# The head of a GRU kernel: the order of its first loads and products

## The chip, the cores and the metric

The kernel runs on one core of one Trainium2 chip. The metric is device time in microseconds (us) from the start to the end of one launch; the smaller the better. A profile of one execution is at hand beside the times.

## The reference

A recurrent network (a GRU cell) runs over 256 time steps for a batch of 16 sequences of width 512; its states then go through an expert layer with a router, and the result is added to the input. Cut to what matters here:

```python
def cell(h, x):                       # 256 times, one after the other
    gi = x @ W_ih + b_ih              # known for all steps ahead of time
    gh = h @ W_hh + b_hh              # needs the state of the step before
    i_r, i_z, i_n = jnp.split(gi, 3, axis=-1)
    h_r, h_z, h_n = jnp.split(gh, 3, axis=-1)
    r = jax.nn.sigmoid(i_r + h_r)
    z = jax.nn.sigmoid(i_z + h_z)
    n = jnp.tanh(i_n + r * h_n)
    return (1.0 - z) * n + z * h
# h starts as cond (16 x 512); W_ih and W_hh are 512 x 1536, x is 16 x 256 x 512
# then: logits = hs @ router_w + router_b; softmax over 16 experts; each expert
# takes its 256 best tokens; y adds weight * (token @ expert_w + expert_b)
# result: x + y
```

All tensors are float32.

## The kernel before

**Stages.** The kernel has three: a head that loads the weights and works out the first input products, a loop of 256 recurrence steps, and an end that picks the tokens of each expert and writes the result. The change touches the head alone.

**Layout.** The time steps are cut into 32 groups of 8 (TG = 8, NG = 32); group g of x lies in `xs[:, g]`, 128 rows (16 sequences by 8 steps) of 512 values. W_ih lies in `wih`, four blocks k = 0 to 3 of 128 rows of 1536 values (0.79 MB each, one contiguous row of 6 KB for each partition); W_hh lies in `whh`, loaded by gate (r, z and n are gates 0, 1 and 2; 1 MB each, in pieces of 2 KB). `b_raw` and `b_n` hold the bias vectors, `c0` the first state. Parts of `xs` that are not yet needed serve as room for other things: the bias vectors, the masks' numbers, and sums made from W_ih.

**What the head does on TensorE (PE).** `begin_sums` (L93) multiplies zeros to open six PSUM banks, and two more such products (`keep_clock`, 512 columns each) follow. `spread_x(0)` transposes group 0 (four products with `ident`, L732), and VectorE (DVE) copies the result to `xT[0]` in four parts (L735). Two more `keep_clock` products follow. Then come the input products (L618) of W_ih's blocks k = 0 to 3, for four pairs of time steps each; behind block 1 the transposes of `c0` (L748); behind block 2 the bias products (`biases`, L492: 16 products of one or two rows of ones with the bias vectors, which spread the biases over the partitions) and the transposes of group 1 (L732). After block 3 come the products of two more pairs of steps, one more `keep_clock` product, and the first recurrence products of the loop (L705).

**What the head does on the other engines.** DVE makes the masks (`make_masks`, from numbers that GpSimd (POOL) writes), the copies of x, sums and differences of W_ih's blocks (`mixes`, L645, 1.75 us each at full size), the copy of the biases (L756, L757), and adds the biases to the products (`x_done`, L629). ScalarE (ACT) is used in the head for DMA issues and, at its end, for four small copies.

**Queues.** Three engines issue DMAs: ACT and SP (SyncE) through hardware queues, POOL through a software queue; in the profile they are q10, q1 and q0. ACT issues group 0 of x, blocks 0 and 1 of W_ih, gate 0 of W_hh and three quarters of gate 1. SP issues blocks 2 and 3, group 1 of x, gate 2, the last quarter of gate 1, and group 2 of x in 8 pieces (`load_xa`). POOL issues `cond` and three bias vectors. A one-element POOL write into block 2 (L457) makes SP wait until POOL has come that far.

**What sets the order.** The blocks under `manual_schedule` keep the order in which the code is written, for the engines named there, so each engine runs its instructions in the order of the text and waits by semaphores. A DMA whose issue follows eight or more others also waits for the landing of an earlier one, since eight semaphores go round for the hardware queues.

Of the kernel before, what the change touches and what calls it, by code (L numbers as in the profile page):

```python
# [11 lines left out]
I32 = mybir.dt.int32  # L12
AF = mybir.ActivationFunctionType
ALU = mybir.AluOpType
# [3 lines left out]
def kernel(  # L18
# [15 lines left out]
    nc = tc.nc  # L34
    B, T, D = x.shape
    E = router_w.shape[1]
    P = 128
    QD = 32
    KC = D // P
    TG = P // B  # L40
# [5 lines left out]
    xs = const.tile([P, NG, D], F32, name="xs")  # L46
# [4 lines left out]
    wih = const.tile([P, KC, 3, D], F32, name="wih")  # L51
# [6 lines left out]
    GH = P // E  # L58
# [7 lines left out]
    ones_b = const.tile([P, B], F32, name="ones_b")  # L66
    zero = xs[:, NG - 1, D - P // 2 :].bitcast(BF16)
    nc.gpsimd.memset(zero, 0.0)
    make_identity(nc, ident)

    def make_masks():

        nc.gpsimd.memset(ones_b, 1.0)
        shift = GH.bit_length() - 1
        at = xs[:, 10, 0:3].bitcast(I32)
        nc.gpsimd.iota(at[:, 0:1], pattern=[[0, 1]], base=0, channel_multiplier=1)
        nc.vector.tensor_single_scalar(at[:, 1:2], at[:, 0:1], shift, ALU.logical_shift_right)
        nc.vector.tensor_single_scalar(at[:, 2:3], at[:, 0:1], GH - 1, ALU.bitwise_and)
        at_f = xs[:, 11, 0:3]
        nc.vector.tensor_copy(at_f, at)  # L80
        to_i = xs[:, 11, P : 3 * P].bitcast(I32).rearrange("p (o e h) -> p o e h", o=2, h=GH)
        nc.gpsimd.iota(to_i[:, 0, :, :], pattern=[[1, E], [0, GH]], base=0, channel_multiplier=0)
        nc.gpsimd.iota(to_i[:, 1, :, :], pattern=[[0, E], [1, GH]], base=0, channel_multiplier=0)
        to = xs[:, 10, P : 3 * P].rearrange("p (o n) -> p o n", o=2)
        nc.vector.tensor_copy(to, to_i.rearrange("p o e h -> p o (e h)"))
        nc.vector.tensor_scalar(same_f, to[:, 0, :], at_f[:, 1:2], None, ALU.is_equal)
        nc.vector.tensor_copy(same_h, same_f)
        nc.vector.tensor_scalar(row_of, to[:, 1, 0:GH], at_f[:, 2:3], None, ALU.is_equal)
# [273 lines left out]
    with (  # L362
# [12 lines left out]
        whh = wts.tile([P, KC, 3, D], F32, name="whh")  # L375
        bias = wts.tile([P, 4, P], F32, name="bias")
# [4 lines left out]
        C2 = 3 * P // 2  # L381
        spare = xs[:, RING:, :].rearrange("p g d -> p (g d)")[:, AHEAD * 3 * P : AHEAD * 3 * P + C2]
# [9 lines left out]
        c0 = xs[0:B, 7, :]  # L392
# [18 lines left out]
        def load_xa(g, xa, j, qs):  # L411

            for o in range(2):
                q = QD * j + B * o
                qs[o].dma_start(
                    out=xa[q : q + B],
                    in_=x[:, g * TG + o : (g + 1) * TG : 2, j * P : (j + 1) * P],
                )
# [7 lines left out]
        def new_xa():  # L426
            return xap.tile([P, TG // 2, P], F32, name="xa")
# [12 lines left out]
        with tc.manual_schedule(engines={ET.SP, ET.Activation, ET.Pool}):  # L440
            def load_gate(gate, queue, ks=slice(0, KC)):
                queue.dma_start(
                    out=whh[:, ks, gate, :],
                    in_=w_hh[:, gate * D : (gate + 1) * D].rearrange("(c p) n -> p c n", c=KC)[:, ks, :],
                )

            def load_k(k, queue):
                queue.dma_start(
                    out=wih[:, k].rearrange("p g d -> p (g d)"),
                    in_=w_ih.rearrange("(p c) n -> p c n", c=KC)[:, k, :],  # L450
                )

            nc.scalar.dma_start(out=xs[:, 0, :], in_=x[:, 0:TG, :])
            load_k(0, nc.scalar)
            load_k(1, nc.scalar)
            nc.gpsimd.dma_start(out=c0, in_=cond)
            nc.gpsimd.memset(wih[0:1, 2, 0, 0:1], 0.0)  # L457
            load_k(2, nc.sync)
            load_k(3, nc.sync)
            nc.sync.dma_start(out=xs[:, 1, :], in_=x[:, TG : 2 * TG, :])  # L460
            load_gate(0, nc.scalar)
            load_gate(2, nc.sync)
            load_gate(1, nc.scalar, slice(0, KC - 1))
            load_gate(1, nc.sync, slice(KC - 1, KC))
            xa_next = new_xa()
            for c in range(KC):
                load_xa(2, xa_next, c, (nc.sync, nc.sync))
            nc.scalar.activation(dummy, ones[0:1, 0:1], AF.Sigmoid)
            for dst, src in (
                (b_raw[0:1], b_ih.rearrange("(o g d) -> o g d", o=1, d=D)),  # L470
                (b_raw[1:2], b_hh.rearrange("(o g d) -> o g d", o=1, d=D)),
                (b_n, b_hh[2 * D :].rearrange("(o d) -> o d", o=1)),
            ):
                nc.gpsimd.dma_start(out=dst, in_=src)

        def load_expert(part, s):

# [11 lines left out]
        def biases(bank):  # L489
            for i, rows in enumerate((b_raw[:, 0, :], b_raw[:, 1, :], b_raw[0:1, 2, :], b_n)):  # L490
                for j in range(KC):
                    nc.tensor.matmul(  # L492
                        bank[quadrant(j), P * i : P * (i + 1)],
                        ones[0 : rows.shape[0]],
                        columns(rows, j),
                        start=False,
                        stop=True,
                        tile_position=(0, QD * j),
                        skip_group_check=True,
                    )  # L500
# [216 lines left out]
        def keep_clock(n, banks=idles):  # L717

            for i in range(n):
                begin_sums(banks[i % len(banks)])  # L720

        with tc.manual_schedule(engines={ET.PE, ET.Activation, ET.DVE, ET.Pool}):
            make_masks()
            for bank in banks:
                begin_sums(bank)
            keep_clock(2)
            held = (r_bank, n_bank, z_bank, x_bank0, x_bank1, idles[1])

            def spread_x(g, bank):
                xT[g] = xtp.tile([P, TG // 2, P], F32, name="xt")  # L730
                for c in range(KC):
                    nc.tensor.transpose(bank[:, P * c : P * (c + 1)], xs[:, g, c::KC], ident)  # L732
                for q in range(TG // 2):
                    to = xT[g][:, q, :].rearrange("p (c o b) -> p c o b", c=KC, b=B)
                    nc.vector.tensor_copy(  # L735
                        to, bank.rearrange("p (c b t) -> p c t b", c=KC, t=TG)[:, :, 2 * q : 2 * q + 2, :]
                    )

            spread_x(0, idles[0])
            keep_clock(2, (idles[1],))  # L740
            for k in range(KC):
                for p in range(KC):
                    for gates in (slice(0, 1), slice(1, 3)) if p == k == 0 else (slice(0, 3),):
                        x_part(p, k, held[p], gates, start=False)
                if k == 1:
                    mixes(0)
                    for c in range(KC):
                        nc.tensor.transpose(  # L748
                            idles[0][:, B * c : B * (c + 1)], c0[:, P * c : P * (c + 1)], ident[0:B, 0:B]
                        )  # L750
                    nc.vector.tensor_copy(
                        hs[:, :, 0, :], idles[0][:, 0 : KC * B].rearrange("p (k b) -> p k b", b=B)
                    )
                elif k == 2:
                    biases(l_bank)
                    nc.vector.tensor_copy(bias, l_bank.rearrange("p (g d) -> p g d", d=P))  # L756
                    nc.vector.tensor_tensor(spare, bias_f[:, C2 : 2 * C2], bias_f[:, 0:C2], ALU.subtract)  # L757
                    spread_x(1, idles[0])
                    x_sums(1)
                elif k == 3:  # L760
                    mixes(1)
            for p in range(KC):
                x_done(p, held[p])
                if p == 0:
                    preset_first(0)
                elif p == 2:
                    preset_rest(0)
            for p in (KC, KC + 1):
                for k in range(KC):
                    for gates in (slice(0, 1), slice(1, 3)):  # L770
                        x_part(p, k, held[p], gates, start=False)
                if p == KC:
                    mixes(3)
                x_done(p, held[p])
                if p == KC:
                    nc.scalar.copy(a_sum, bias_f[:, 0:C2])
            keep_clock(HEAD_FILL, (idles[0],))

        first, second = range(KC // 2), range(KC // 2, KC)

        with tc.manual_schedule(engines={ET.PE, ET.Activation, ET.DVE, ET.Pool, ET.SP}):
# [6 lines left out]
            for s in range(T):  # L788
# [25 lines left out]
                n = 0  # L814
# [451 lines left out]
```

## Time and profile before

| | us |
|---|---|
| median of 3 runs (lowest, highest) | 1114.81 (1114.41, 1114.88) |
| the profiled execution: time, and span of its instructions | 1114.45, 1112.6 |
| PE busy | 1101.7 (99%) |
| PE's recurrence products, L705 | 722.1 |
| DVE busy | 802.0 (72%) |
| ACT busy | 579.0 (52%) |
| POOL busy | 30.0 (3%) |
| start of the loop (first L705) in the span | 25.79 |

The span goes from the first to the last instruction that the profile shows. PE is busy nearly throughout; the granted TensorE clock is 0.998 of full speed over the span. In the first fortieth of the span the DMA engines are busy 7 tenths and move 258 GB/s, in the second 63 GB/s: the head is the stage that loads. Line numbers (L618) are those of the kernel before; where the changed kernel is meant, the text says so.

### The profile page before, as it was taken

The page shows a single profiled execution, that of the slowest core. Times are in us where ns is not written, and L with a number is a line of the kernel's source. Part 1 is how long each engine was busy: PE and PEld are TensorE (multiplying, and loading weights), DVE is VectorE, ACT ScalarE, POOL GpSimd, SP SyncE. Part 2 cuts the span into 40 slices and gives each one's busy share as a digit, 9 for nine tenths or more (in the row PEclk, how much of TensorE's full clock was granted, in tenths as well). Part 3 has the DMA queues.
Part 4 walks back from the last instruction along what each step waited for, and adds up shares of the span by engine and source line. Part 5 has one row for each costly group of instructions (what it writes and reads, how often), then busy time and mean ns, then how long its engine had stood idle before and what let it go on. Part 6 is the DMA issues. An engine that isn't in the chain of part 4 may idle for free.

```text
span 1112.6 us, 77160 instructions
## 1 busy us (share of the span) xinstructions
PE 1101.7 (99%) x34291; PEld 957.8 (86%) x34291; DVE 802.0 (72%) x4664; ACT 579.0 (52%) x2644; POOL 30.0 (3%) x173
## 2 busy tenths in 40 slices
PE   9999999999999999999999999999999999999998
PEld 4888888888888888888888888888888888888763
DVE  4777666776777676767767677777777777777786
ACT  1555555555555555555555555555555555554551
POOL 1000000000000000000000000000000000000000
PEclk9999999999999999999999999999999999999999
DMA  7200000000000000000000000000000000002437
GB/s 258 63 11 12 12 12 14 19 21 21 21 21 12 12 14 14 14 14 12 12 12 12 14 14 14 14 12 12 12 12 14 14 15 14 4 4 80 136 108 238
DMA packets 34371, 37.34 MB, mean 34 GB/s; under 512 B 6112, under 2 KB 23776, under 8 KB 34032
## 3 DMA queue, kind: packets, MB, share of 16 engines
q1 hardware_dynamic: 32544, 28.64, 8.9%
q8 instruction: 270, 4.42, 1.6%
q10 hardware_dynamic: 1360, 3.67, 0.9%
q14 instruction: 69, 0.57, 0.2%
q0 software_dynamic: 128, 0.05, 0.0%
HBM read 23.94 MB, written 8.39 MB: 29 GB/s over the span
## 4 chain that ended last, share of the span: by engine, by line
PE 93%; DVE 4%; ACT 1%; DMA 1%; issue 0%; ACTq 0%; DVEq 0%
PE gates L705 59%; PE x L678 20%; PE gates L678 4%; PE pe L586 3%; PE x L308 3%; PE pe L308 2%; PE pe L115 1%; DVE nT L897 1%; DMA wih<-in_L_cond_W_ih_dram 1%; DVE t L859 1%; DVE zT L900 1%; PE gates L618 1%; ACT r L798 1%; ACT t L863 1%; PE x L618 0%
## 5 line engine op out<-in xcount | busy, mean ns | idle before, releaser
L705 PE MATMUL gates<-whh,hs 128*16 128x128 f32 x24576 | 722.1, 273 | 3.1 <-DVE hs L911 2.4
L705 PEld LDWEIGHTS gates<-whh,hs 128*16 128x16 f32 x24576 | 652.0, 103 | 57.0 <-DVE hs L911 50.5
L798 ACT ACTIVATE r<-gates 128x128 f32<-128x128 f32 x256 | 70.9, 277 | 232.8 <-PE gates L705 232.8
L802 DVE COPY seen<-r 1x1 f32<-1x1 f32 x256 | 36.3, 142 | 199.7 <-ACT r L798 199.4
L900 DVE STREAM_TRANSPOSE zT<-zs 128x32 f32<-128x32 f32 (+1 forms) x768 | 165.7, 216 | 0.0
L863 ACT ACTIVATE t<-t 128x64 f32<-128x64 f32 x512 | 103.1, 248 | 104.2 <-DVE t L861 104.2
L897 DVE STREAM_TRANSPOSE nT<-t 128x64 f32<-128x64 f32 x512 | 100.2, 234 | 48.1 <-ACT t L863 48.1
L908 DVE TENSOR_TENSOR v<-u,zT 128x32 f32<-128x32 f32 x512 | 98.7, 193 | 8.8
L911 DVE TENSOR_TENSOR hs<-v,nT 128x32 f32<-128x32 f32 x512 | 95.4, 186 | 8.7
L678 PE MATMUL x<-wih,xt 128*32 128x192 f32 (+2 forms) x1968 | 101.7, 325 | 0.0
L861 DVE TENSOR_TENSOR t<-t,xs 128x64 f32<-128x64 f32 x512 | 90.8, 220 | 0.0
L678 PE MATMUL x<-wih,xs 128*32 128x192 f32 x1952 | 90.5, 326 | 0.0
L859 DVE TENSOR_TENSOR t<-r,gates 128x64 f32<-128x64 f32 x512 | 90.3, 218 | 0.0
L865 ACT ACTIVATE zs<-gates 128x64 f32<-128x64 f32 x512 | 86.6, 221 | 0.0
L903 DVE TENSOR_TENSOR u<-hs,nT 128x32 f32<-128x32 f32 x512 | 78.3, 153 | 0.0
L678 PEld LDWEIGHTS x<-wih,xt 128*32 128x32 f32 x1968 | 62.4, 110 | 11.8
L678 PEld LDWEIGHTS x<-wih,xs 128*32 128x32 f32 x1952 | 62.2, 110 | 11.9
L511 ACT COPY ht<-hs 128x128 f32<-128x128 f32 (+1 forms) x128 | 52.0, 408 | 0.7 <-DVE hs L911 0.7
L678 PE MATMUL x<-xs 128*32 128x192 f32 (+1 forms) x1040 | 50.9, 316 | 0.0
L678 PE MATMUL x<-xs,xt 128*32 128x192 f32 x976 | 50.8, 326 | 0.0
L678 PE MATMUL gates<-xs 128*32 128x192 f32 x976 | 50.8, 326 | 0.0
L881 ACT COPY x<-x 128x192 f32<-128x192 f32 x61 | 18.5, 303 | 62.0 <-PE x L678 62.0
(199 smaller groups left out, 938.6 us busy)
## 6 DMA issues: line engine op xcount, KB each, us to landing
out_dram<-xs SPq DMA_DIRECT2D x31, 256.0 KB, 3.7
xa<-in_x_dram SPq DMA_DIRECT2D x240, 32.0 KB, 2.9
xs<-in_x_dram SPq DMA_DIRECT2D x27, 256.0 KB, 4.1
wih<-in_L_cond_W_ih_dram ACTq DMA_DIRECT2D x2, 768.0 KB, 6.4
wih<-in_L_cond_W_ih_dram SPq DMA_DIRECT2D x2, 768.0 KB, 9.6
whh<-in_L_cond_W_hh_dram ACTq DMA_DIRECT2D x1, 1024.0 KB, 15.7
whh<-in_L_cond_W_hh_dram SPq DMA_DIRECT2D x1, 1024.0 KB, 17.8
ewr<-in_L_ffn_expert_w_dram SPq DMA_DIRECT2D x4, 256.0 KB, 3.0
```

What stands on the lines that cost most here:

```text
L678: nc.tensor.matmul(dst[quadrant(j), at:to], lhs[:, QD * k : QD * (k + 1)], columns(rows[k], j)[:, at // QD : to // QD], start=False, stop= ...
L705: nc.tensor.matmul(dst[quadrant(j, m)], lhs, columns(whh[:, k, gate_, :], j), start=False, stop=(k == KC - 1), tile_position=(0, QD * j), ...
L798: nc.scalar.activation(r, rr[p % 2], AF.Sigmoid)
L859: nc.vector.tensor_tensor(t[half], r[:, cols], hn[p % 2][:, cols], ALU.mult)
L861: nc.vector.tensor_tensor(t[half], t[half], ring[:, p % AHEAD, 2, cols], ALU.add)
L863: nc.scalar.activation(t[half], t[half], AF.Tanh)
L865: nc.scalar.activation(zs[half], zz[p % 2][:, cols], AF.Sigmoid)
L897: nc.vector.transpose(nT[half], t[half])
L900: nc.vector.transpose(zT[half][:, part], zs[half][:, part])
L903: nc.vector.tensor_tensor(u[half], hs[:, halves[half][2], slot(s), :], of_step(nT[half], odd), ALU.subtract)
L908: nc.vector.tensor_tensor(v[half], u[half], of_step(zT[half], odd), ALU.mult)
L911: nc.vector.tensor_tensor(hs[:, halves[half][2], slot(s + 1), :], v[half], of_step(nT[half], odd), ALU.add)
```

## The change

The change moves loads, products and mask work about within the head:

- ACT's queue carries both first groups of x and all four blocks of W_ih in order, then gate 0 of W_hh.
- SP's queue carries gates 1 and 2 of W_hh, whole, and group 2 of x. A one-element POOL copy from block 0 of `wih` to gate 1's place in `whh` stands ahead of them, so SP waits until block 0 has landed.
- POOL issues the bias vectors first and `cond` last.
- The numbers for the masks are written in a function of their own (`number`) on POOL, after its DMA issues; the mask work on DVE (`make_masks`) moves from the start of the head to behind the copies of group 0.
- The bias products, the copy of the biases and the difference made from them move from behind block 2 to ahead of block 0.
- The two `keep_clock` products ahead of block 0 are left out; two of 16 columns each stand ahead of the last `keep_clock` product of the head.

```diff
+    shift = GH.bit_length() - 1
+    at = xs[:, 10, 0:3].bitcast(I32)
+    at_f = xs[:, 11, 0:3]
+    to_i = xs[:, 11, P : 3 * P].bitcast(I32).rearrange("p (o e h) -> p o e h", o=2, h=GH)
+    to = xs[:, 10, P : 3 * P].rearrange("p (o n) -> p o n", o=2)
+
+    def number():
+
+        nc.gpsimd.iota(at[:, 0:1], pattern=[[0, 1]], base=0, channel_multiplier=1)
+        nc.gpsimd.iota(to_i[:, 0, :, :], pattern=[[1, E], [0, GH]], base=0, channel_multiplier=0)
+        nc.gpsimd.iota(to_i[:, 1, :, :], pattern=[[0, E], [1, GH]], base=0, channel_multiplier=0)
+        nc.gpsimd.memset(ones_b, 1.0)
+
     def make_masks():
 
-        nc.gpsimd.memset(ones_b, 1.0)
-        nc.gpsimd.iota(at[:, 0:1], pattern=[[0, 1]], base=0, channel_multiplier=1)
...
             nc.scalar.dma_start(out=xs[:, 0, :], in_=x[:, 0:TG, :])
-            load_k(0, nc.scalar)
-            load_k(1, nc.scalar)
-            nc.gpsimd.dma_start(out=c0, in_=cond)
-            nc.gpsimd.memset(wih[0:1, 2, 0, 0:1], 0.0)
-            load_k(2, nc.sync)
-            load_k(3, nc.sync)
-            nc.sync.dma_start(out=xs[:, 1, :], in_=x[:, TG : 2 * TG, :])
+            for k in range(3):
+                load_k(k, nc.scalar)
+            nc.scalar.dma_start(out=xs[:, 1, :], in_=x[:, TG : 2 * TG, :])
+            load_k(3, nc.scalar)
             load_gate(0, nc.scalar)
-            load_gate(2, nc.sync)
-            load_gate(1, nc.scalar, slice(0, KC - 1))
-            load_gate(1, nc.sync, slice(KC - 1, KC))
-            xa_next = new_xa()
-            for c in range(KC):
-                load_xa(2, xa_next, c, (nc.sync, nc.sync))
-            nc.scalar.activation(dummy, ones[0:1, 0:1], AF.Sigmoid)
             for dst, src in (
                 (b_raw[0:1], b_ih.rearrange("(o g d) -> o g d", o=1, d=D)),
                 (b_raw[1:2], b_hh.rearrange("(o g d) -> o g d", o=1, d=D)),
                 (b_n, b_hh[2 * D :].rearrange("(o d) -> o d", o=1)),
             ):
                 nc.gpsimd.dma_start(out=dst, in_=src)
+            nc.gpsimd.dma_start(out=c0, in_=cond)
+            number()
+            nc.gpsimd.tensor_copy(whh[0:1, 0, 1, 0:1], wih[0:1, 0, 0, 0:1])
+            load_gate(1, nc.sync)
+            load_gate(2, nc.sync)
+            xa_next = new_xa()
+            for c in range(KC):
+                load_xa(2, xa_next, c, (nc.sync, nc.sync))
+            nc.scalar.activation(dummy, ones[0:1, 0:1], AF.Sigmoid)
...
-            make_masks()
             for bank in banks:
                 begin_sums(bank)
             keep_clock(2)
...
             spread_x(0, idles[0])
-            keep_clock(2, (idles[1],))
+            make_masks()
+            biases(l_bank)
+            nc.vector.tensor_copy(bias, l_bank.rearrange("p (g d) -> p g d", d=P))
+            nc.vector.tensor_tensor(spare, bias_f[:, C2 : 2 * C2], bias_f[:, 0:C2], ALU.subtract)
...
                 elif k == 2:
-                    biases(l_bank)
-                    nc.vector.tensor_copy(bias, l_bank.rearrange("p (g d) -> p g d", d=P))
-                    nc.vector.tensor_tensor(spare, bias_f[:, C2 : 2 * C2], bias_f[:, 0:C2], ALU.subtract)
                     spread_x(1, idles[0])
                     x_sums(1)
...
                 if p == KC:
                     nc.scalar.copy(a_sum, bias_f[:, 0:C2])
+            keep_clock(2, (idles[0][:, 0:E],))
             keep_clock(HEAD_FILL, (idles[0],))
```

More of the change, by code (lines that the diff above doesn't have):

```diff
@@ L69 @@
     make_identity(nc, ident)
+    shift = GH.bit_length() - 1
[8 more added lines that the diff above has]
+        nc.gpsimd.memset(ones_b, 1.0)
     def make_masks():
-        nc.gpsimd.memset(ones_b, 1.0)
-        shift = GH.bit_length() - 1
-        at = xs[:, 10, 0:3].bitcast(I32)
-        nc.gpsimd.iota(at[:, 0:1], pattern=[[0, 1]], base=0, channel_multiplier=1)
         nc.vector.tensor_single_scalar(at[:, 1:2], at[:, 0:1], shift, ALU.logical_shift_right)
         nc.vector.tensor_single_scalar(at[:, 2:3], at[:, 0:1], GH - 1, ALU.bitwise_and)
-        at_f = xs[:, 11, 0:3]
         nc.vector.tensor_copy(at_f, at)
[L81 to L84, printed above, removed]
         nc.vector.tensor_copy(to, to_i.rearrange("p o e h -> p o (e h)"))
```

## The prediction

> **What bounds the kernel now.** I read the page first: PE is busy 99% of the span and its recurrence products (L705, 722.1 us) fill the loop. The diff changes no instruction of the loop, and the changed kernel's queues list the same instructions in the same order from the loop's first product on. So only the time at which the loop begins can move. That I read from the chain of waits of the first 60 us (start, length, what):
>
> ```profile
> 2.07 7.90 DMA wih<-in_L_cond_W_ih_dram
> 9.97 0.04 issue
> 10.01 2.14 PE gates L618 x24
> ...
> 15.86 1.01 PE gates L492 x32
> ...
> 25.47 0.32 PE idle L93
> 25.79 1.48 PE gates L705 x48
> ```
>
> Block 1 of w_ih lands at 9.97. From 10.01 PE runs without a hole to the loop at 25.79, 15.78 us, and the bias products (L492) take 1.01 of them. Before 10.01, the timeline of PE (start, length; in brackets the idle time and what ended it):
>
> ```profile
> 4.45 1.10 PE L732 MATMUL idle<-ident,xs 128*128 128x128 f32 x4
> 5.34 1.06 PE L93 MATMUL idle<-xs 128*128 128x512 bf16 x2
> 6.44 2.21 PE L618 MATMUL gates<-wih,xt 128*32 128x128 f32 x32
> ...
> 10.01 2.14 PE L618 MATMUL gates<-wih,xt 128*32 128x384 f32 x24 [0.72 <-DMA wih<-in_L_cond_W_ih_dram]
> ...
> 25.40 0.39 PE L93 MATMUL idle<-xs 128*128 128x512 bf16 x1
> ```
>
> Block 0's products start at 6.44, a moment after block 0 lands (issued 1.44, 4.9 us on its way: 6.3); they last 2.02 us to the first x product at 8.46 and 0.65 more, 2.67 in all. Then PE waits 0.72 for block 1. So the most the head could give is the wait and the bias products, 0.72 + 1.01 = 1.73 us.
>
> Next, how long POOL's small loads take, from the DMA issues of the first 45 us (last number: us from issue to landing):
>
> ```profile
> xs<-in_cond_dram POOLq DMA_DIRECT2D x1, 32.0 KB, 3.2
> xs<-in_L_cond_b_ih_dram POOLq DMA_DIRECT2D x1, 6.0 KB, 5.7
> xs<-in_L_cond_b_hh_dram POOLq DMA_DIRECT2D x1, 6.0 KB, 6.4
> xs<-in_L_cond_b_hh_dram POOLq DMA_DIRECT2D x1, 2.0 KB, 6.5
> ```
>
> POOL issued them at 1.34, 2.32, 2.82 and 3.30, so the bias vectors landed at 8.0, 9.2 and 9.8: after block 0. Why 6 KB need 5.7 us: the DMA queues in the stretch from 7 to 8 us (packets, MB, share):
>
> ```profile
> q1 hardware_dynamic: 33, 0.20, 49.5%
> q10 hardware_dynamic: 32, 0.20, 47.8%
> q0 software_dynamic: 34, 0.01, 3.6%
> ```
>
> The three queues (SP's, ACT's, POOL's) send equal numbers of packets: 16 engines take turns, two rounds in this us, some 0.45 to 0.5 us each, though POOL's packets are tiny. From 4.5 to 5.5 us ACT's queue alone sent 69 packets, 0.41 MB (4.3 rounds, 0.23 us each): one queue alone keeps the rate.
>
> Last, the groups by shape, of the first 6.4 us, of 6.43 to 6.46, and of the rest of the head (count | busy, mean ns):
>
> ```profile
> L93 PE MATMUL idle<-xs 128*128 128x512 bf16 x4 | 2.1, 634 | 0.0
> ...
> L618 PE MATMUL gates<-wih,xt 128*32 128x128 f32 x3 | 0.4, 357 | 0.0
> ...
> L93 PE MATMUL idle<-xs 128*128 128x512 bf16 x1 | 0.4, 389 | 0.0
> ```
>
> The same 512-column product takes 634 ns up to 6.4 us and 389 at 25.4; block 0's first takes 357 where its later ones take 273. PE thus came to full speed during block 0's first products, about 6.6, though the granted clock reads 1.00 from the start. The two fillers at 5.34 lie just ahead of that.
>
> **The change, part by part.** *w_ih in order on ACT's queue.* Block 0 has no other queue beside it before or after: 6.3. At 0.4 MB a us each further block (0.79 MB) needs 2 us: block 1 at some 8.3 instead of 9.97, block 2 at 10.3, the second x group about 11. The last block shares engines with the released queue. In 9.5 to 11.5 us of before, 6 KB rows against 2 KB rows moved 0.60 against 0.23 MB, so it gets some 0.3 MB a us and lands about 14. Removed: the 0.72 us wait, if PE needs block 1 no earlier than 8.3.
>
> *SP held.* POOL's one-element copy waits for block 0 (6.3); copies of this kind take 0.17; SP issues gate 1's weights (0.4), gate 2's, and the 8 loads of group 2, at about 6.6 instead of 4.3 for its gate. Behind the copy on POOL stands only a copy that waits for the first state, as before. The bytes are the same, and before they were all there at 23.1 (6.3 + 16.8 for the last piece of gate 1); the loop needs gates 0 and 2 at once. I count it at nothing: 3 us of cover. Group 2 is turned only at 34.95.
>
> *Bias products ahead.* They leave the chain between 10 and 25.8 (-1.01) and become the first thing PE does after the transposes, which end at 5.45. Everything of x now waits behind them, and they wait for all three vectors. POOL now issues b_ih at 1.34 (0.50), the identity's select (0.30), then b_hh at 2.2 and its n part at 2.7. Below: with cond's 3.2 us they land at 5.4 and 5.9. Above: with their own 6.4 and 6.5, at 8.6 and 9.2. I take a value between: b_hh is issued where b_ih was (2.32, landed 8.0), and each vector costs each of 16 engines two packets (POOL's queue has 128 on the page, for four loads), but a round is now one 6 KB row, 0.25 us, instead of two. Two rounds 0.2 shorter and 0.1 earlier: 7.5; two rounds more for the n part: 8.0. The first three quarters of the products (0.76) then end at 8.26, the rest (0.25) at 8.51. Block 0's products start at 8.5 instead of 6.44.
>
> *Masks behind the x copies on DVE, POOL's numbering apart.* The seven mask operations (4.01 to 5.58) go behind the four copies of x and before the bias copy (0.69 + 0.36): DVE is then idle until the bias products end, so nothing. cond is issued last on POOL, at 3.2; it is needed after block 1, past 13.
>
> *Fillers.* Two 512-column fillers leave a wait (nothing, but for the clock below); two of 16 columns come before the last one: 0.09 each by the four 16-column transposes (0.35), 0.32 each by the 512-column one. I take 0.2 together.
>
> **Sum.** Block 0 starts at 8.51; then 2.67, then 15.78 - 1.01 = 14.77, then 0.2: the loop starts at 26.15 instead of 25.79, **+0.36 us**. DVE's run after the second group's transposes keeps its place relative to PE. By the bounds of the vectors: landed by 5.9, block 0 starts at 6.5 and the loop at 24.14 (-1.65); landed at 8.6 and 9.2, block 0 starts at 9.61 (+1.46). The profiled execution took 1114.45 (span 1112.6 and 1.85 around it), 0.36 under the median of 1114.81. So 1114.45 + 0.36 = 1114.81 for one like it, and **1115.2** for the median.
>
> [...] In the rows, PE came to full speed at 6.6, after 5.6 us of which it was busy in about 5.2. [...]
>
> **Rivals.**
> 1. *The vectors come early*, like cond, since only one queue is beside them: -1.65, 1113.2. For it: b_ih has cond's slot. Against: b_hh still meets block 0's 6 KB rows, as b_ih did at 2.32. 15%.
> 2. *The slow clock* (the other side): without the two fillers PE is idle for 2 us just where full speed came. Slow fillers follow each other by 1.06 - 0.63 = 0.43 us, 0.83 ns a column; 634 - 389 = 245 ns less for 512 leaves 0.35 at full speed, so slow is about twice as long. Before, that fell into waits. If full speed again takes 5.6 us from 7.5, half of that is lost: 2.8, with the 0.36 together 1118.0; if the work before 5.45 counts and 2 us suffice, 1.0: 1116.2. Middle 1117.1. It decides from the point where full speed comes later than 7.5. For it: 634 against 389. Against: PE is busy from 1.00 to 5.45. 30%.
> 3. *The vectors or the held gates are late.* Vectors as slow as before: 1116.3. Gates decide only if they land after 26.5, over 3 us later than now. 7%.
> The forecast has 45%, its own range 1114.6 to 1116.0; 3% is for what I don't see.
>
> **How the numbers follow.** 0.2%, about what a measurement of this kernel can tell from no change, is 2.2 us. Rival 1 ends short of that: faster has 4%, for the unseen and a still shorter head. The upper half of rival 2 and part of rival 3 go beyond it: slower 22%. The rest is 74%. The range goes from near rival 1 to near the far end of rival 2: 1113.4 to 1117.9.
>
> **What would show it.** Block 0's first product (L618) at about 8.5, released by the bias products, and no wait for blocks 1 to 3 after it; the vectors' landings at 7.5 and 8.0; the 128-column products of block 0 at 273 ns. Rival 2: 384-column products well above 486 ns after 7.5. Rival 1: block 0 at 6.5. Wrong at the root: a stall between 8.5 and 26 for w_ih or w_hh, or loop steps other than 3.96 us apart.

## The result and the profile after

| | before | after |
|---|---|---|
| median of 9 runs of each (lowest, highest), us | 1114.6 (1114.22, 1115.36) | 1117.89 (1116.43, 1118.5) |
| ratio of the times, 95% interval | | 1.0027, 1.0017 to 1.0038 |
| profiled execution, its span, us | 1114.45, 1112.6 | 1117.71, 1115.8 |
| first L705 (before), L708 (after), us in the span | 25.79 | 28.78 |
| from there to the end of the span, us | 1086.8 | 1087.0 |

The kernel became 3.3 us slower. (A few lines more stand ahead of these in the changed kernel: L618, L492, L705, L732 and L93 of before are L621, L495, L708, L734 and L97 now.) The last row says where to look: the loop and what follows take the same time, and the loop begins 2.99 us later. So 2.99 of the 3.2 us by which the span grew were lost in the head.

The chain of waits of the first 60 us of after (start, length, what):

```profile
2.28 5.01 DMA xs<-in_L_cond_b_hh_dram
7.43 1.93 PE gates L495 x32
9.36 4.00 PE gates L621 x32
13.36 0.81 PE x L621 x8
14.16 1.94 PE gates L621 x24
...
28.41 0.37 PE idle L97 x3
28.78 1.48 PE gates L708 x48
```

The chain now begins with the load of b_hh, where it began with block 1 of w_ih. From its landing PE has no hole up to the loop. Two links are longer than they should be: the bias products take 1.93 us, against 1.01 in the chain of before, and block 0 takes 4.00 + 0.81 = 4.81, against 2.67. That is 0.92 + 2.14 = 3.06 us, as much as the loop's start moved.

The timeline of PE in after shows what stands ahead of them:

```profile
4.39 1.06 PE L734 MATMUL idle<-ident,xs 128*128 128x128 f32 x4
7.43 1.93 PE L495 MATMUL gates<-xs,ones 2*32 2x128 f32 x32 [1.98 <-DMA xs<-in_L_cond_b_hh_dram]
9.29 4.07 PE L621 MATMUL gates<-wih,xt 128*32 128x128 f32 x32
13.13 1.03 PE L621 MATMUL x<-wih,xt 128*32 128x384 f32 x8
13.99 2.11 PE L621 MATMUL gates<-wih,xt 128*32 128x384 f32 x24
```

PE is idle for 1.98 us until 7.43. Then 32 products of block 0 (L621; 8 of 128 columns, 8 of 256 and 16 of 384) last 4.07 us, while 24 of block 1, all of 384 columns and so the same number of columns in all, last 2.11. To see whether block 0 did more work or slower work, take the groups by shape, of after from 7.4 to 13.1 us (count | busy, mean ns of one | idle before):

```profile
L621 PE MATMUL gates<-wih,xt 128*32 128x384 f32 x16 | 2.8, 847 | 0.0
L495 PE MATMUL gates<-xs,ones 1*32 1x128 f32 x16 | 1.1, 415 | 0.0
L621 PE MATMUL gates<-wih,xt 128*32 128x256 f32 x8 | 1.1, 634 | 0.0
L495 PE MATMUL gates<-xs,ones 2*32 2x128 f32 x16 | 1.1, 414 | 2.0 <-DMA xs<-in_L_cond_b_hh_dram 2.0
L621 PE MATMUL gates<-wih,xt 128*32 128x128 f32 x8 | 0.7, 422 | 0.0
```

and of before from 6.9 to 9.9 us:

```profile
L618 PE MATMUL gates<-wih,xt 128*32 128x384 f32 x16 | 1.5, 486 | 0.0
```

The same 16 products of 384 columns took 847 ns each instead of 486; they overlap (16 of 847 ns would be 13.6 us one after the other), so their busy time shows it better, 2.8 against 1.5 us. The 24 products of block 1 in after are back at 486 ns. So PE ran slow up to some 13.5 us, where before it came to full speed at 6.6. The page's clock row says nothing of it, since the clock record in the trace begins only with full speed, at 6.62 in before and at 13.55 in after. These moments are called the grant below.

The loads came nearly as forecast. From the DMA issues of the first 45 us of after (last number: us from issue to landing):

```profile
xs<-in_L_cond_b_ih_dram POOLq DMA_DIRECT2D x1, 6.0 KB, 3.0
xs<-in_L_cond_b_hh_dram POOLq DMA_DIRECT2D x1, 6.0 KB, 5.0
xs<-in_L_cond_b_hh_dram POOLq DMA_DIRECT2D x1, 2.0 KB, 5.5
```

The vectors landed at 4.39, 7.29 and 8.24. The first moved beside group 0 of x. From 4 to 6 us, while the rest of block 0 came in, ACT's queue alone moved packets (queue: packets, MB, share of the engines' time):

```profile
q10 hardware_dynamic: 146, 0.80, 100.6%
```

The other two vectors moved only behind that, beside block 1, as the queues from 6 to 8 us show:

```profile
q10 hardware_dynamic: 139, 0.76, 96.7%
q0 software_dynamic: 95, 0.04, 7.4%
```

### The profile page after: what moved, and what is told of

Read it like the earlier page. It is cut to its first block, busy times and chain, and to the rows that moved or that the text cites. A ratio compares the mean times of both kernels' runs of the same rounds, so it can differ in the third digit from the quotient of the medians.

```text
span 1115.8 us, 77160 instructions
## 1 busy us (share of the span) xinstructions
PE 1103.5 (99%) x34291; PEld 958.8 (86%) x34291; DVE 801.9 (72%) x4664; ACT 579.1 (52%) x2644; POOL 30.2 (3%) x173
## 4 chain that ended last, share of the span: by engine, by line
PE 93%; DVE 4%; ACT 1%; DMA 0%; issue 0%; POOL 0%; POOLq 0%; DVEq 0%; ACTq 0%
PE gates L708 59%; PE x L681 20%; PE gates L681 3%; PE pe L589 3%; PE x L312 3%; PE pe L312 2%; PE pe L119 1%; PE gates L621 1%; DVE nT L900 1%; DVE t L862 1%; DVE zT L903 1%; ACT r L801 1%; ACT t L866 1%; PE x L621 0%; DMA xs<-in_L_cond_b_hh_dram 0%
## 5 line engine op out<-in xcount | busy, mean ns | idle before, releaser
L708 PE MATMUL gates<-whh,hs 128*16 128x128 f32 x24576 | 722.1, 273 | 3.1 <-DVE hs L914 2.4
L708 PEld LDWEIGHTS gates<-whh,hs 128*16 128x16 f32 x24576 | 652.0, 103 | 57.0 <-DVE hs L914 50.5
```

The source lines that it names most:

```text
L708: nc.tensor.matmul(dst[quadrant(j, m)], lhs, columns(whh[:, k, gate_, :], j), start=False, stop=(k == KC - 1), tile_position=(0, QD * j), ...
```

## The experiments

A median is compared with that of the kernel before on the same chip. "Loop" is the first recurrence product in the timeline of the kernel's one profile; there it starts at 25.72 in before and at 28.71 in after, 0.07 ahead of the chain, which counts from the end of the product before.

| kernel | median (lowest, highest), us | before there | ratio, 95% | grant, loop in the profile, us |
|---|---|---|---|---|
| fillers in the wait | 1115.84 (1115.15, 1117.73) | 1115.04 | 1.0008, 0.9998 to 1.0019 | 3.83, 26.33 |
| queues alone | 1114.14 (1113.99, 1115.69) | 1115.04 | 0.9994, 0.9985 to 1.0003 | 4.40, 24.68 |
| vectors on SP | 1114.3 (1113.18, 1116.9) | 1115.04 | 0.9996, 0.9987 to 1.0005 | 4.32, 23.77 |
| before without fillers | 1115.85 (1114.71, 1117.09) | 1115.04 | 1.0006, 0.9997 to 1.0015 | 10.22, 26.65 |
| after again | 1118.75, one run | 1114.6 | | 13.59, 28.96 |
| two-row fillers | 1115.24 (1113.8, 1117.53) | 1114.6 | 1.0004, 0.9996 to 1.0013 | 10.17, 26.55 |
| SP, full rows | 1118.41 (1116.12, 1122.17) | 1114.6 | 1.0032, 1.0019 to 1.0046 | 13.77, 29.20 |
| queues, no hold | 1119.24 (1119.18, 1120.12) | 1114.6 | 1.0039, 1.0026 to 1.0052 | 14.98 (second), 31.13 |
| SP and fillers | 1113.24 (1112.8, 1116.4) | 1113.87 | 0.9996, 0.9987 to 1.0005 | 4.78, 24.20 |
| queues again | 1113.21 (1112.91, 1113.61) | 1113.87 | 0.9995, 0.9986 to 1.0004 | 4.30, 24.66 |
| fillers again | 1116.29, one run | 1113.87 | | 12.47 (second), 28.07 |

Most of these differences are near or under what their intervals tell apart. What the experiments settle rests on the profiles of the head, where half a microsecond is plain. What follows the loop's start takes 1086.4 to 1088.7 us in the thirteen profiles.

### After with fillers in the wait

```diff
             spread_x(0, idles[0])
+            keep_clock(5, (idles[1],))
             make_masks()
             biases(l_bank)
```

If PE is slow because it stands idle before the bias products, products of zeros in that wait should bring back the forecast's sum; if the vectors' lateness alone costs the time, they change nothing.

> The changed kernel with five 512-column fillers between the transposes of group 0 and the bias products, so that PE has work while it waits for the vectors. Theory A (the clock: PE idle from 5.45 to 7.43 keeps the array slow up to 13.4, and the bias products then take 1.93 instead of 1.01 us and block 0 4.81 instead of 2.67): full speed comes before block 0, its 128-column products take 273 ns, bias products from 7.4 to 8.4, loop at 26.0, time within 0.7 us of the kernel before. Rival B (the place of the bias products and the wait for the vectors cost it, whatever the clock): the loop begins at 28 or later, 2 to 3 us over the kernel before.

The timeline of PE in its profile:

```profile
7.98 1.09 PE L495 MATMUL gates<-xs,ones 2*32 2x128 f32 x32 [1.78 <-DMA xs<-in_L_cond_b_hh_dram]
8.99 2.15 PE L621 MATMUL gates<-wih,xt 128*32 128x128 f32 x32
...
26.33 2.81 PE L708 MATMUL gates<-whh,hs 128*16 128x128 f32 x96
```

The wait for the vectors is still there, and b_hh landed even later, at 7.84. But the bias products last 1.09 instead of 1.93 and block 0's 32 products 2.15 instead of 4.07. The loop begins at 26.33, 26.40 in the chain, where the forecast's sum had put it at 26.15. So the late vectors cost about what was forecast, and the rest of the loss is PE's speed.

The grant in this profile came at 3.83, ahead of the fillers, which start at 4.95: they didn't bring full speed here, they can only have kept it. That they do so in part of the runs, the times suggest: none of the ten runs of after lies under 1116.43, and six of 11 here do. The times fall in two groups, six of 11 runs at 1115.15 to 1115.84 and five at 1117.29 to 1117.73; the profile is of the first. What the second is, the last experiment shows.

### The queues alone

The bias products, the copy and the difference go back behind block 2, and the two fillers back ahead of block 0; the new order of the loads stays.

```diff
             spread_x(0, idles[0])
+            keep_clock(2, (idles[1],))
             make_masks()
-            biases(l_bank)
-            nc.vector.tensor_copy(bias, l_bank.rearrange("p (g d) -> p g d", d=P))
...
                 elif k == 2:
+                    biases(l_bank)
+                    nc.vector.tensor_copy(bias, l_bank.rearrange("p (g d) -> p g d", d=P))
```

> The changed kernel with the bias products back behind block 2 and the two fillers back ahead of block 0: the new order of the loads alone. Theory A: block 0 starts at 6.2 to 6.4 and takes 2.7, blocks 1 to 3 are there when PE comes to them, so the 0.72 us wait is gone and the loop begins at 24.9 to 25.1, 0.7 to 0.9 us before that of the kernel before (time 1113.8). Rival C (the new order of the loads or the held queue costs it): a wait for w_ih or w_hh shows, and the loop begins at 25.8 or later.

Run a second time on another chip:

> e2 again (new order of the loads, bias products behind block 2, two fillers ahead of block 0), beside the kernel before and e9 on one chip. Theory A: loop at 24.7 in most executions, 0.7 to 1.0 us under the kernel before; close together, since the fillers reach up to block 0.

The timeline of PE in the second one's profile:

```profile
6.32 2.15 PE L621 MATMUL gates<-wih,xt 128*32 128x128 f32 x32 [0.75 <-DVE xs L87]
...
8.90 2.15 PE L621 MATMUL gates<-wih,xt 128*32 128x384 f32 x24
...
24.66 2.81 PE L708 MATMUL gates<-whh,hs 128*16 128x128 f32 x96
```

Block 1 starts at 8.90 with no wait, where it stood at 10.01 behind a wait of 0.72 us. The loop begins some 1.05 us earlier than before in both profiles, the medians are 0.90 and 0.66 us lower, and the second series lies within 0.7 us, the narrowest of all series of five runs or more; the first spans 1.7. Both profiles show the grant before block 0 (4.40 and 4.30) and kept from there on (the clock reads 1.00 up to 16 us). By the ratios it is some 3.6 to 3.7 us (1.0027 less 0.9994 or 0.9995) faster than after, on other chips; against before, both intervals still reach past 1, so a gain of two thirds of a microsecond is likely and not proved.

### The bias vectors on SP's queue

```diff
-                nc.gpsimd.dma_start(out=dst, in_=src)
+                nc.sync.dma_start(out=dst, in_=src)
```

On SP's queue, ahead of what waits for block 0, the vectors have nothing in front of them; the wait of PE should go without any filler.

> The changed kernel with the three bias vectors issued by SP ahead of its hold instead of by POOL. Theory A: the vectors land before 5.4, PE has no idle time between the transposes and the bias products, full speed comes near 6.6 as before, block 0 starts near 7 and the loop at 24.1 to 24.8: 1.0 to 1.7 us faster than the kernel before. Rival B: the bias products ahead of block 0 cost time even with the vectors there: loop at 26 or later. Rival: the vectors in front delay group 0 of x (landing after 4.2), and the loop by as much.

With the two fillers in as well:

> e3 (bias vectors by SP ahead of its hold) with the two fillers of 512 columns back, ahead of the bias products. Theory A (clock): PE does full-row work up to 5.4 or 6.1, so fewer executions miss the stretch that brings full speed; where it came early, block 0 starts at 6.5 to 6.7 and the loop at 24.0, median 1113.2 to 1113.8, or 1 us under the kernel before, with fewer runs above 1115 than e3 had (4 of 11). If fillers do nothing here: as e3, median 0.7 under the kernel before and the same spread.

The timeline of PE in the first one's profile:

```profile
5.19 1.08 PE L495 MATMUL gates<-xs,ones 2*32 2x128 f32 x32
6.43 2.15 PE L621 MATMUL gates<-wih,xt 128*32 128x128 f32 x32 [0.16 <-DVE xs L87]
```

The bias products run from 5.19 to 6.27, block 0 from 6.43, and the loop begins at 23.77, 1.95 us earlier than before; this is the early end of the forecast (24.14) come true, and more. Yet the median is only 0.74 us lower, and 4 of its 11 runs lie above 1115.7. With the two fillers, which push block 0 back to 6.87, two of 11 lie above 1115, and the median is 0.63 lower. So early vectors make the shortest head, when the clock plays along, and it seems to do so only in some executions; no slow run was profiled.

### Before, without its two fillers

```diff
             spread_x(0, idles[0])
-            keep_clock(2, (idles[1],))
             for k in range(KC):
```

This takes the fillers alone away from the kernel before and moves nothing.

> The kernel before without the two fillers ahead of block 0, nothing else. Theory A: PE idle from 5.45 to 6.4 loses the stretch that ends at 6.6; full speed comes near 10.0 or 13.4, block 0's 128-column products take about 420 ns, the loop begins at 26.6 to 28.0: 0.8 to 2.2 us slower. Rival B: the fillers only filled a wait; the loop begins at 25.8, the same time.

The timeline of PE:

```profile
6.59 3.92 PE L618 MATMUL gates<-wih,xt 128*32 128x128 f32 x32 [1.08 <-DMA wih<-in_L_cond_W_ih_dram]
...
10.96 2.12 PE L618 MATMUL gates<-wih,xt 128*32 128x384 f32 x24
```

Two products of zeros, left out where PE waits anyway, make block 0's products last 3.92 us instead of 2.21; the grant comes at 10.22. The expectation's 10.0 was the author's estimate; the step that a later profile shows, 3.41 us from one change of the clock to the next, puts it at 10.03 from the 6.62 of before. A part of that falls into the old wait for block 1, which is gone from the timeline; the loop begins 0.93 later, and the median is 0.81 higher. The profiled execution is the slowest of the 11 (1117.09); behind the loop's start it took 1.8 us more than the profile of before, so the time of this one run is no measure of the fillers, the start of its loop is.

### After, once more

One profile of the changed kernel as it is, on another chip.

> The changed kernel once more, for a second profile: four profiles so far saw full speed come at 13.4, 3.8, 4.4 and 4.3 us, so the moment differs from one execution to the next. Theory A: whichever way it falls, block 0's first products take about 420 ns, either because full speed has not come before the idle stretch from 5.3 to 7.4, or because it came and was taken back over it; a mean granted clock of 0.996 would be the second (about 9 us at half speed on record). If it came early and stays, loop at 26. Rival B: products at 273 ns and the loop still at 28 or later.

```profile
7.91 1.93 PE L495 MATMUL gates<-xs,ones 2*32 2x128 f32 x32 [2.45 <-DMA xs<-in_L_cond_b_hh_dram]
```

The timeline has the slow bias products again, 1.93, and block 0's 32 products take 4.01. The grant at 13.59 lies beside the 13.55 of the first profile. The expectation's other way is in the times of after: five of its nine runs, 1117.78 to 1118.5, have a mean granted clock of 0.996. The slow clock on record is half speed: it reads 0.50 from 1109.2 to the end of the span in before. So that is some 9 us of it (0.004 x 1116 x 2, an estimate), of which the end of the launch has at most 4.4 in the profiles. In these runs full speed probably came early and was taken back, and they are as slow; none of them was profiled.

### Do products of two rows count?

The bias products multiply one or two rows where all others multiply 128. In the kernel before, the two fillers were cut to two rows:

```diff
-            keep_clock(2, (idles[1],))
+            for _ in range(2):
+                nc.tensor.matmul(
+                    idles[1], zero[0:2], zero[0:2, 0:E].unsqueeze(1).to_broadcast([2, D // E, E]), start=True, stop=True
+                )
```

> The kernel before with its two fillers ahead of block 0 cut to two rows (of 128) of the array, as the bias products have, with the same columns and so the same time on PE. Theory A1 (products of two rows don't count as work for the clock): like the kernel before without these fillers, 0.6 to 1.0 us slower, single runs from 1114.7 to 1117. Theory A2 (any product counts): as the kernel before, most runs between 1114.7 and 1115.3.

The timeline of PE:

```profile
4.43 1.10 PE L732 MATMUL idle<-ident,xs 128*128 128x128 f32 x4
5.47 1.03 PE L741 MATMUL idle<-xs 2*128 2x512 bf16 x2
6.45 3.96 PE L618 MATMUL gates<-wih,xt 128*32 128x128 f32 x32
```

The fillers fill the same time, 1.03 us against 1.06, and PE has no hole from 1.00 on. Still block 0 ran slow, as with no fillers at all: grant at 10.17, against 10.22 there and 6.62 before. The medians are no judge, since the interval of this one holds both no change and the 0.81 us of the kernel without fillers. One profile speaks strongly for two-row products not counting as work for the clock; it is one execution.

The other way round, bias products over all 128 rows (vectors on SP's queue, the rows that are not loaded set to zero by DVE):

```diff
-        b_raw = xs[0:2, 3:6, :]
-        b_n = xs[0:1, 6, :]
+        b_raw = xs[:, 3:6, :]
+        b_n = xs[:, 6, :]
...
-        ones = wts.tile([2, QD], F32, name="ones")
+        ones = wts.tile([P, QD], F32, name="ones")
+        nc.vector.memset(xs[:, 3:6, :].rearrange("p g d -> p (g d)").bitcast(BF16), 0.0)
+        nc.vector.memset(xs[:, 6, :].bitcast(BF16), 0.0)
```

> The changed kernel with the bias vectors issued by SP ahead of its hold, into rows that DVE has set to zero, so that the bias products use all 128 rows of the array: same columns, same time on PE. Theory A1: the slow half of e3's runs (1115.7 to 1116.9) goes away; median 1113.3 to 1113.8, 1.2 to 1.8 us faster than the kernel before. Theory A2: as e3, median 1114.3 and single runs up to 1117. If the zeros delay the vectors past 5.4, block 0 starts later than 6.5 by as much.

This one gave no answer. SP's loads had to wait for the zeros, were issued at 2.5 to 3.2 us and landed late, so PE was idle for 2.82 us up to 8.36, longer than in after. It went slow like after (bias products 1.93, grant 13.77), and nothing follows for the rows.

### Without the hold on SP

From the queues alone, the POOL copy that keeps SP until block 0 is there was left out.

```diff
             number()
-            nc.gpsimd.tensor_copy(whh[0:1, 0, 1, 0:1], wih[0:1, 0, 0, 0:1])
             load_gate(1, nc.sync)
```

> e2 (the new order of the loads, bias products behind block 2, fillers kept) without POOL's copy that holds SP's queue: gates 1 and 2 start at once. Theory A with equal turns of the queues: from about 6 us SP's 2 KB rows take turns with ACT's 6 KB rows, block 1 gets three quarters of the rate and lands near 9.2, block 2 near 12, block 3 near 16 or later; PE waits a few tenths for block 1 and for block 3, loop at 25.0 to 25.6, time 1114.3 to 1114.9. If the hold does nothing: 1114.1, loop at 24.7. If the hold itself costs: earlier than 24.7.

It missed what was expected by far: 1119.24, 4.6 us above before. The timeline of PE:

```profile
7.70 0.83 PE L733 MATMUL idle<-ident,xs 128*128 128x128 f32 x4 [3.11 <-DMA xs<-in_x_dram]
8.33 1.06 PE L97 MATMUL idle<-xs 128*128 128x512 bf16 x2
10.70 4.07 PE L620 MATMUL gates<-wih,xt 128*32 128x128 f32 x32 [1.31 <-DVE row_of L92]
```

The windows of the same profile (stretch; its length, busy time of PE, PEld, DVE, ACT, POOL; PEclk, DMA share, GB/s):

```profile
8.00:12.00 4.00, 2.69 (x26) 1.35 (x28) 2.02 (x11) 0.00 (x0) 0.00 (x0) 0.52 1.03 386
12.00:16.00 4.00, 4.00 (x36) 1.47 (x32) 1.76 (x1) 0.00 (x0) 0.00 (x0) 0.63 1.03 375
```

SP's issue of gate 1's weights ended at 1.20, ACT's of group 0 of x at 1.41. From 3 to 5 us its queue moved 347 packets and ACT's 17: gate 1 landed at 7.26 and group 0 of x at 7.57, instead of 4.3. PE stood idle for 3.11 us in the transposes' place, block 0 landed at 10.56, and the clock, granted early at 4.74, was taken back from 8.16 to 14.98 (0.52 and 0.63 in the windows). Late loads and slow clock together put the loop at 31.13, 6.5 us later than with the hold. So the hold, whose delay of SP's loads the forecast had counted at nothing, is what makes the new order work.

### Fillers in the wait, once more

One profile of the first experiment's kernel on another chip, to see its second group.

> e1 again (the changed kernel with five fillers before the bias products), for a second profile. In e1 six runs lay at 1115.2 to 1115.8 and five at 1117.3 to 1117.7 with a mean clock of 0.997 to 0.998. Theory A: in a run of the second kind full speed comes before 7 and is taken back when the stretch with PE idle (about 6.2 to 8) ends; block 0's products then take about 420 ns. In a run of the first kind: as e1's profile, loop at 26.3.

It is that group: 1116.29, 2.4 us over before there. The timeline of PE, and the windows of the same profile:

```profile
5.24 1.45 PE L97 MATMUL idle<-xs 128*128 128x512 bf16 x5
8.08 1.08 PE L495 MATMUL gates<-xs,ones 2*32 2x128 f32 x32 [1.39 <-DMA xs<-in_L_cond_b_hh_dram]
9.09 3.79 PE L621 MATMUL gates<-wih,xt 128*32 128x128 f32 x32
```

```profile
4.00:8.00 4.00, 2.69 (x11) 1.34 (x9) 2.02 (x11) 1.49 (x2) 0.67 (x4) 1.00 1.01 392
8.00:12.00 4.00, 3.92 (x60) 2.22 (x64) 2.72 (x3) 0.00 (x0) 0.00 (x0) 0.63 1.02 348
12.00:16.00 4.00, 4.00 (x48) 1.28 (x40) 0.00 (x0) 0.00 (x0) 0.00 (x0) 0.94 1.03 387
```

The bias products ran at full speed here, 1.08. Then, with PE busy, block 0 went slow, 3.79: full speed had been granted at 5.64, was taken back at 9.05, just as block 0 began, and came again at 12.47. Both stretches are some 3.41 us long, and in the first PE was idle for 1.39 us and on two-row products for 0.97. So in this profile it is not idleness at the moment that goes with a slow block 0; what PE did in the 3.41 us up to there is what is left. In the first experiment's profile, granted at 3.83, stretches of that length, put end to end, would end at 7.24 and 10.65: its gap of 1.78 us fell on both, 1.04 and 0.74, and full speed stayed. By these two profiles, the two groups of times are two positions of the same gap.

## Why the prediction was wrong in its choice and right in one of its rivals

*The landings, right.* The forecast had b_hh at 7.5 and the n part at 8.0; they came at 7.29 and 8.24. By these, at full speed, block 0 would have begun at 8.49, against the forecast's 8.51. The way there was another than the forecast's turns between POOL's rows and block 0's: from 4 to 6 us POOL's queue moved nothing, in before as in after. The number held since the row that it was worked out from (issued at 2.32, landed at 8.0) had that wait in it. "The vectors come early" didn't happen on POOL's queue; on SP's it did.

*W_ih in order, right.* Blocks 0 to 3 landed at 6.07, 8.44, 10.56 and 14.37 (forecast 6.3, 8.3, 10.3, 14), group 1 of x at 11.74 (11). No product waits for any of them, and the wait of 0.72 is gone. The queues alone show the new order to be worth 1.05 us of head: block 0 starts 0.1 earlier, and the wait was worth more than 0.72. From the start of block 0 to that of block 1 there were 3.57 us in before for 2.67 of products, so 0.90; the most that the head could give was nearer 1.9 than 1.73, as the vectors on SP show with 1.95.

*SP held, right in its cost, incomplete in its worth.* POOL's copy ran at 6.13, after 1.63 us of waiting for block 0, and SP issued at 6.33. Gates 0, 1 and 2 landed at 21.21, 19.29 and 23.73; the loop's first product waits for none. What the forecast didn't ask is what SP's loads would do without it: 6.5 us of harm in one profile.

*Masks and numbering, right.* DVE's mask work ran from 6.29 to 7.6, in the shade of PE's wait; the copy of the biases followed at 9.42.

*The fillers at the end, oversized.* They lengthened that run from 0.32 to 0.37, 0.05 for the 0.2 forecast. The stretch from block 1 to the loop took 14.62 us instead of 14.97: 0.15 of the gain is this, and the other 0.20 is the link of block 1 in the chain, 1.94 instead of 2.14, now that no wait stands ahead of it.

*The step that failed* is "Two 512-column fillers leave a wait (nothing, but for the clock below)", with the sum made at full speed from the first bias product on. With them, by these profiles, went a condition for full speed: in the stretch that ends near 6.7 PE was busy for 2.14 us of 3.42 in after, and for 3.37 of 3.41 in before (the lines are shown below), and taking the fillers alone from the kernel before gives the same slow block 0. The terms in its place: bias products +0.92, block 0 +2.14, vectors -0.07, the rest -0.35, together 2.64; 26.15 + 2.64 is 28.79, and the loop began at 28.78. The slow clock, kept as a rival at 30% and priced at 1116.2 to 1118.0, is what happened, in the upper part of its bounds (1117.89): its worst case lost half of 5.6 us, and 3.06 us were lost. So the measured time lies 2.7 us above the forecast's 1115.2, at the very end of the range 1113.4 to 1117.9, and beyond the 2.2 us from which on the forecast called it slower, at 22%; that the range still holds it is this rival's doing, not the sum's.

*Where its weight was wrong.* Against the rival stood "PE is busy from 1.00 to 5.45". The profiles show that this is not enough. (In before PE was busy for 5.40 us up to 6.4, not for about 5.2 up to 6.6, as the forecast has it.) Reckoned back from the grants in steps of 3.41 us (the step measured in the last experiment; that it holds ahead of a grant is an estimate), a stretch ends between 6.6 and 6.8 us in five of them, so these can be compared although the grant lies elsewhere in each execution. The windows of these stretches, in the order before, after, after again, before without fillers, two-row fillers (stretch; its length, busy time of PE; PEclk, DMA share, GB/s; the clock is 1.00 here for want of a record):

```profile
3.21:6.62 3.41, 3.37 (x14) 1.00 1.02 377
3.31:6.73 3.42, 2.14 (x8) 1.00 0.99 381
3.35:6.76 3.41, 2.11 (x7) 1.00 1.02 398
3.39:6.80 3.41, 2.33 (x12) 1.00 0.98 369
3.34:6.75 3.41, 3.41 (x17) 1.00 1.03 381
```

Only before, where products of 128 rows fill the stretch, has its grant at the end of it. The two kernels with no fillers or with two-row fillers have it one stretch later, at 10.22 and 10.17. In after the next stretch holds the rest of the wait and the two-row bias products, and the grant comes two later, at 13.55 and 13.59. The far bound of rival 2, full speed after 5.6 us more from 7.5, so at 13.1, and 2.8 + 0.36 = 3.16 us in all, came near: 13.55, and 2.99 at the loop's start.

*What the traces show of the clock.* In the last experiment's profile grant, loss and new grant are 3.41 us apart (5.64, 9.05, 12.47); without the hold they are 3.42 and 6.82 apart (4.74, 8.16, 14.98), one step and two. With the other profiles the first grant lies anywhere from 3.83 to 13.77. In six profiles it came by 4.78, ahead of the products in which the kernels differ. So, as far as these profiles go, the moment at which a step ends is the execution's, and what the kernel decides is how busy PE is in the steps. A gap's length alone does not tell what follows: one of 1.39 us, inside such a stretch and with 0.97 us of two-row products behind it, went with the loss of full speed, and gaps of 0.75 us beside 128-row products (the queues alone, both profiles) did not. In the kernel with two-row fillers PE had no gap at all for 9.2 us before its grant, so a stretch of 3.41 us without a hole, if the steps run through, ended by 7.82 at the latest (1.00 and two steps) and brought nothing.

*Open.* What counts as activity: that products of two rows don't fits every profile here, but the run meant to give the counterproof gave no answer, and the two-row fillers have one profile. How much of a stretch must be busy is not known either. With the two-row products left out, the stretches that ended without a grant were busy for up to 74% of their length, and the least busy one that ended with a first grant for 83% (2.83 of 3.41 us, fillers in the wait). Full speed once granted was kept over a stretch with 2.26 us busy (the same profile, from 3.83 on) and lost over one with 2.02, of them 0.97 on two-row products (fillers again, from 5.64 on).

## What to carry to other kernels

A filler product that sits in a wait may still hold up time: here two of them, about 1 us of nothing, were worth 0.9 us of head in one profile of the kernel before (0.8 in the medians, near what their interval tells apart). Five in the longer wait of after went with a loop at 26.33 instead of 28.71 in one profile, and with short times in only about half the runs. Before moving a product ahead of its data at the start of a kernel, ask what TensorE does meanwhile, and price every product behind the wait at slow speed too, which an early slow product of the same shape in the trace gives (in before 634 ns up to 6.4 us against 389 at 25.4 for 512 columns). When one queue is to deliver in order, hold back the queues that carry what is needed later (without the hold the loop began 6.5 us later here), and judge changes of a head over many runs, since the moment of full speed differs between executions of the same kernel (3.83 and 5.64 in the two profiles with fillers in the wait).

## What was not expected of the hardware

Full speed, once granted, was taken back after a stretch with only 1.39 us without products and 0.97 on two-row ones, for 3.41 us (9.05 to 12.47, fillers again), while PE was already busy again. In two cases here a queue whose load was issued first did not share from the start. Without the hold, SP's gate kept ACT's smaller load, whose issue ended 0.2 us later, out until about 4.5 us, 347 packets to 17 between 3 and 5 us; and while block 0 came in, POOL's queue moved nothing from 4 to 6 us, in before and after (140 and 146 packets on ACT's queue), though the three queues sent equal numbers of packets in before from 7 to 8 us (33, 32 and 34). So a load of 6 KB took 3.0 us as the first of POOL's queue and 5.0 as the second, and the order within that queue decided when PE could begin.
